# Where the long product of heads 0 and 1 stands in a visit's scores

## The chip, the cores and the metric

The kernel runs on one core of a Trainium2 chip. The metric is the time of one execution on the device in microseconds; lower is better. The engines are TensorE (PE in the profile, its weight loads PEld), VectorE (DVE), ScalarE (ACT), GpSimd (POOL) and SyncE (SP, which issues DMAs).

## The reference

```python
# x: (32, 256, 32, 32) float32, S = 1024 tokens, 8 heads of 32 channels
def reference(x, L0_conv_q_w, L0_conv_q_b, L0_conv_kv_w, L0_conv_kv_b):
    def _L0_conv_ref(x, q_w, q_b, kv_w, kv_b):
        ...
        q = jnp.einsum('oc,bcs->bos', q_w, xf) + q_b[None, :, None]
        kv = jnp.einsum('oc,bcs->bos', kv_w, xf) + kv_b[None, :, None]
        k, v = (kv[:, :EMBED_C], kv[:, EMBED_C:])
        ...
        mask = jnp.tril(jnp.ones((S, S), dtype=x.dtype), -int(MASK_CENTER))
        scores = jnp.einsum('bhqd,bhkd->bhqk', q, k) / jnp.sqrt(jnp.asarray(dk, x.dtype))
        scores = jnp.where(mask == 0, jnp.asarray(-10000.0, x.dtype), scores)
        attn = jax.nn.softmax(scores, axis=-1)
        attn = jnp.where(mask == 0, jnp.asarray(0.0, x.dtype), attn)
        out = jnp.einsum('bhqk,bhkd->bhqd', attn, v)
        ...
    # _gn: group norm over 32 groups of 8 channels
    x = x + _L0_conv_ref(_gn(x), L0_conv_q_w, L0_conv_q_b, L0_conv_kv_w, L0_conv_kv_b)
    return x
```

A group norm, three projections, strictly causal attention with 8 heads over 1024 tokens, and the residual, for 32 batch elements, all in float32.

## The kernel before

One element of the batch (called a batch below, b) has two groups g of four heads, and each group's attention is worked off in six visits i, so a batch has twelve visits, numbered v = 6g + i. A visit takes a part of the causal triangle: keys on the partitions, queries along the columns. `VISITS[i]` says which: one or two long products (rectangles, up to 512 queries wide) and, as a short one, either a pair of diagonal blocks (`pair`, in visits 0, 1, 3 and 4, which `PAIRS` lists) or one more rectangle of 256 queries (visits 2 and 5). Visits 0 and 5 have two long products, 384 and 128 wide; 1, 2, 3 and 4 have one, 512 wide. A pair consists of two products for each half of the keys, one 128 and one 64 wide.

The scores of one head have a contraction of only 32 channels, so `score` (L329, tile `sT`) uses a 32x64 part of the TensorE array: the rows of the array are the head's, and the two halves of a block's 128 keys go to different columns of it. Four heads and two halves are eight such parts. Each float32 matmul stands twice in the trace, as two passes. In all of the order's listings below, `x4` is two heads by two halves.

A visit has three PSUM tiles `sT`, numbered 0, 1 and 2 at the end of their names: 0 takes the long products of heads 0 and 1, 1 those of heads 2 and 3, and 2 the short products of all four, heads 2 and 3 in the same banks as heads 0 and 1. Two matmuls must not write one bank from different rows of the array at once, so the short products are made for heads 2 and 3 first, their last matmuls count up the semaphore `bank_free`, and TensorE waits for it ahead of the short products of heads 0 and 1.

The order is written out by hand (the pools and semaphores come from a tile framework, each engine's instructions stand as the code issues them): for each visit its scores, then parts of the projections (`pp`, `ppv`, L173), then the products with the values of the visit before (`acc`, L451). ScalarE takes the exponentials of the three `sT` tiles (L426, L426, L422) in the order 0, 1, 2; GpSimd masks the pairs; VectorE adds the exponentials up for the sums of the softmax.

In `scores` the list `begin` holds what is made of the long products of heads 0 and 1 before those of heads 2 and 3. `scores_of` calls its argument `between` between the first and the second product of a pair, and goes through the pair backwards (64 wide first) if told to by `order`. Before the change, `between` is used for heads 2 and 3 only where `begin` has more than one entry: in visit 0, whose two long products are two entries, and, in all batches but the last, in v = 3 and 4 (`SPLIT`), where `part_of` makes the one long product in two cuts of 128 and 384 queries. In the visits v = 1, 7, 9 and 10, and in 3 and 4 of the last batch, both products of the pair come first and then the long one.

Of the kernel before, what the change touches and what calls it, by code (L numbers as in the profile page):

```python
# [32 lines left out]
def tile_norm_attention_residual(  # L33
# [69 lines left out]
    def unshifted():  # L103
# [230 lines left out]
        def scores_of(b, g, bank_of, heads, entries, between=lambda: None, order=slice(None)):  # L334

            done = {}
            for _, _, halves in entries:
                for k, n in enumerate(list(range(max(map(len, halves))))[order]):
                    if k:
                        between()  # L340
                    for j in heads:
                        for c, ops in enumerate(halves):
                            if n < len(ops):
                                done.setdefault((j, c), []).append(score(b, g, bank_of(j), j, ops[n]))
            return done

        def part_of(b, g, bank, entry, of):

            at, _, halves = entry
            for j in (0, 1):  # L350
                for ((c, kb, first, _, cols),) in halves:
                    score(b, g, bank[:, j, :], j, (
                        c, kb, first + of.start, of.stop - of.start, slice(cols.start + of.start, cols.start + of.stop)
                    ))

        def mask(b, g, raw, j):


            hf, place = j // 2, (2 * j % 4) * P
            if ("e", b, g, "D", hf) not in live:  # L360
                live["e", b, g, "D", hf] = epool.tile(
                    [P, 4, HALF], F32, tag=("e0", "e")[hf], bufs=4, name=f"diagonal_{b}_{g}_{hf}"
                )
            square = live["e", b, g, "D", hf]
            for s in range(2):
                nc.gpsimd.affine_select(  # L366
                    out=square[:, :, place + s * P : place + (s + 1) * P],
                    in_=raw[:, :, (1 - s) * KEYS : (3 - s) * KEYS],
                    pattern=[[0, 4], [(1, -1)[s], P]], compare_op=ALU.is_gt, fill=0.0, base=0,
                    channel_multiplier=(-1, 1)[s],  # L370
                )
            if j == 0:
                nc.gpsimd.memset(square[0:1, :, 0:1], 1.0)

        def scores(b, v):


            g, i = divmod(v, len(VISITS))
            longs, shorts = VISITS[i]
            name = f"{b}_{g}_{i}"  # L380
            e = epool.tile([P, 4, HALF], F32, tag="e0" if i == TOTAL else "e", bufs=4, name=f"e_{name}")
            eh = epool.tile([P, 4, HALFBANK], F32, tag="eh", bufs=3, name=f"eh_{name}")
            pairs = [ps_s.tile([P, 2, HALF], F32, tag="sT", name=f"sT_{name}_{a}") for a in range(3)]
            short = pairs[2].rearrange("p bank (n q) -> p bank n q", n=2)
            short_of = lambda heads, *how: scores_of(
                b, g, lambda j: short[:, j % 2, j // 2, :], heads, shorts, *how
            )
            long_of = lambda heads, n: scores_of(b, g, lambda j: pairs[j // 2][:, j % 2, :], heads, longs[n : n + 1])
            rest = [lambda: long_of((2, 3), 1)] if len(longs) > 1 else []
            begin = [lambda n=n: long_of((0, 1), n) for n in range(len(longs) - 1, -1, -1)]  # L390
            if b < B - 1 and v in SPLIT:
                begin = [lambda n=n: part_of(b, g, pairs[0], longs[0], n) for n in (slice(0, P), slice(P, HALF))]
            if i in PAIRS and len(begin) > 1:
                first = short_of((2, 3), begin.pop(0), slice(None, None, -1))
            else:
                first = short_of((2, 3))
            for f in begin:
                f()
            long_of((2, 3), 0)

            ends = [made[-1] for made in first.values()]
            first = [ins for made in first.values() for ins in made]
            for ins in ends:
                ins.then_inc(bank_free, 1)
            for ins in first:
                tc.no_tile_sem_insts.add(ins.ins.name)
            live["free"] = live.get("free", 0) + len(ends)
            wait = nc.tensor.wait_ge(bank_free, live["free"])
            for ins in first:
                tc.declare_no_dep(wait.ins, ins.ins, reason="the semaphore orders them")  # L410
            made = short_of((0, 1), *rest if i in PAIRS else ())
            if i not in PAIRS:
                for f in rest:
                    f()
            for made in made.values():
                for lo in made:
                    for ins in first:
                        tc.declare_no_dep(lo.ins, ins.ins, reason="the semaphore orders them")
            wide, narrow = (max(at + width for at, width, _ in entries) for entries in (longs, shorts))
            for a in range(3):  # L420
                if a == 2:
                    exp = nc.scalar.activation(  # L422
                        eh.rearrange("p (n bank) q -> p bank n q", n=2)[:, :, :, :narrow], short[:, :, :, :narrow], AF.Exp
                    )
                else:
                    nc.scalar.activation(e[:, 2 * a : 2 * a + 2, :wide], pairs[a][:, :, :wide], AF.Exp)  # L426

            for ins in first:
                tc.add_to_no_dep_group(f"first_{name}", ins.ins)
                tc.add_to_no_dep_group("first", ins.ins)  # L430
            tc.declare_no_dep(exp.ins, group=f"first_{name}", reason="through the last two products")
            tc.declare_fence(exp.ins, group=f"first_{name}")
            live["e", b, g, "L", i], live["e", b, g, "H", i] = e, eh
            if i in PAIRS:
                mask(b, g, eh, PAIRS[i])
# [183 lines left out]
        ]  # L619
        N, TOTAL = NG * len(VISITS), 2  # L620
        PAIRS = {0: 0, 1: 1, 3: 3, 4: 2}
        SPLIT = 3, 4

        PRODUCTS = [
            (0, [
# [65 lines left out]
        with tc.manual_schedule(engines={ENG.PE, ENG.Activation, ENG.DVE, ENG.Pool, ENG.SP}):  # L691
# [47 lines left out]
            for b in range(B):  # L739
                first, last = b * N, b == B - 1  # L740
# [44 lines left out]
            for i in range(B * N + 1):  # L785
                if i < B * N:
                    scores(*divmod(i, N))
                for f in at.pop(i, ()):
                    f()
                b, v = divmod(i - 1, N)  # L790
                if i == B * N:

                    sums(3, SUMMED[v], False)
                if i:
                    for _ in range(EVEN.count((i - 1) % N) if i < B * N - N else 0):
                        nc.tensor.wait_ge(bank_free, live["free"])
                    values(b, v)
                    if b < B - 1 or v not in SUMMED or v == 1:
                        add_keys(b, v)
                if i in (B * N - 2, B * N - 1):  # L800

                    sums(3, SUMMED[v])
                for f in after.pop(i, ()):
                    f()
# [9 lines left out]
    def shifted():  # L814


        with ExitStack() as inner:
# [34 lines left out]
            with tc.For_i(0, B, 1) as b:  # L852
# [93 lines left out]
                )  # L946

    inside = unshifted()
    ALL = 3 * P * ROW
    held = nc.values_load(  # L950
# [29 lines left out]
```

## Time and profile before

| | us |
|---|---|
| median of 3 runs | 1791.41 (1791.25 to 1792.9) |
| the profiled execution, from its first instruction to its last | 1791.2 |
| TensorE busy in it | 1782.1 (99%) |
| VectorE busy | 1669.4 (93%) |
| ScalarE busy | 1441.4 (80%) |
| GpSimd busy | 897.9 (50%) |
| one batch in the middle (stretch 957.88 to 1012.86) | 54.98 |

The page gives no other time of the profiled execution than its span, which is 0.2 us below the median of the runs. Busy time of TensorE is the union of matmuls that overlap in the array, so 99% says that some matmul was always in flight, not that the array was full.

### The profile page before, as it was taken

Reading aid. Unit: us, or ns where it says so; the run is one execution under the profiler, and the core shown is the slowest. Engines: PE = TensorE matmul, PEld = TensorE weight load, DVE = VectorE, ACT = ScalarE, POOL = GpSimd, SP = SyncE. Lnnn points to the kernel's source line nnn. Section 1 sums busy time; section 2 is a strip of 40 time slices with the busy share of each in tenths; the row PEclk is TensorE's granted clock in tenths of the full one; section 3 lists DMA queues with packets and bytes.
Section 4 is the critical chain, followed back from the end, with each engine's and each line's share of the span. In section 5 each row is a group of like instructions: output and inputs, shape, how many; then the busy total and the mean of one; then the engine's idle time right before and its main releaser. Section 6 shows DMA issues by size and latency. Waiting matters only on the chain.

```text
span 1791.2 us, 81784 instructions
## 1 busy us (share of the span) xinstructions
PE 1782.1 (99%) x37036; PEld 936.1 (52%) x37036; DVE 1669.4 (93%) x1796; ACT 1441.4 (80%) x1928; POOL 897.9 (50%) x935
## 2 busy tenths in 40 slices
PE   9999999999999999999999999999999999999998
PEld 5555555555555555555555555555555555555554
DVE  4689999999999999999999999999999999999998
ACT  6888878888778788788887888877888878888785
POOL 2355554554555555545555555454455554554542
PEclk9999999999999999999999999999999999999999
DMA  2567766767677676676776676767766766777663
GB/s 72 105 117 142 137 133 135 148 138 147 128 142 138 137 141 138 132 144 142 142 138 134 137 142 138 150 129 140 139 145 131 141 136 135 149 138 141 133 109 98
DMA packets 92771, 240.21 MB, mean 134 GB/s; under 512 B 26272, under 2 KB 27792, under 8 KB 76544
## 3 DMA queue, kind: packets, MB, share of 16 engines
q0 software_dynamic: 17360, 100.58, 40.1%
q1 hardware_dynamic: 74912, 134.28, 25.9%
q8 instruction: 290, 4.75, 1.1%
q14 instruction: 65, 0.53, 0.1%
q10 hardware_dynamic: 144, 0.07, 0.0%
HBM read 69.90 MB, written 34.95 MB: 59 GB/s over the span
## 4 chain that ended last, share of the span: by engine, by line
PE 99%; DVE 0%; ACT 0%; issue 0%; POOL 0%; POOLq 0%
PE sT L329 31%; PE acc L451 28%; PE pp L173 27%; PE ppv L173 13%; PE pd L503 1%; PE busy L159 0%; PE wt L152 0%; ACT e L426 0%; DVE rb_last L576 0%; DVE rb_last L563 0%; DVE turned L560 0%; DVE acc L573 0%; DVE inv_last L562 0%; POOL ident masks.py:199 0%; PE pv L173 0%
## 5 line engine op out<-in xcount | busy, mean ns | idle before, releaser
L426 ACT ACTIVATE e<-sT 128x1024 f32<-128x1024 f32 x768 | 744.3, 1022 | 301.5 <-PE sT L329 298.8
L366 POOL TENSOR_SCALAR_AFFINE_SELECT diagonal<-eh 128x512 f32<-128x512 f32 x512 | 563.3, 1122 | 625.4 <-ACT eh L422 624.7
L469 DVE TENSOR_TENSOR e<-e,e 128x1024 f32<-128x1024 f32 x314 | 578.0, 1841 | 23.0 <-ACT v L293 3.5
L329 PE MATMUL sT<-q,k 32*64 32x64 f32 (+1 forms) x18928 | 577.9, 367 | 0.1
L329 PEld LDWEIGHTS sT<-q,k 32*64 32x64 f32 x18928 | 397.0, 131 | 203.8 <-PE sT L329 67.4
L173 PE MATMUL pp<-xn,wT 128*32 128x512 f32 x4096 | 492.3, 598 | 0.0
L451 PE MATMUL acc<-e,v 128*32 128x512 f32 (+3 forms) x4608 | 401.0, 450 | 0.0
L422 ACT ACTIVATE eh<-sT 128x768 f32<-128x768 f32 (+1 forms) x384 | 341.6, 890 | 0.0
L451 PEld LDWEIGHTS acc<-e,v 128*32 128x32 f32 x4608 | 149.2, 110 | 261.5 <-issue 239.0
L173 PE MATMUL ppv<-wT,xn 128*32 128x256 f32 x4096 | 247.5, 382 | 0.0
L469 DVE TENSOR_TENSOR diagonal<-diagonal,e 128x1536 f32<-128x1536 f32 x126 | 194.5, 1544 | 16.1 <-PE acc L451 6.5
L173 PEld LDWEIGHTS pp<-xn,wT 128*32 128x32 f32 x4096 | 107.0, 109 | 195.8 <-issue 163.7
L469 DVE TENSOR_TENSOR e<-e,eh 128x1024 f32<-128x1024 f32 x126 | 177.6, 1410 | 6.5
L451 PEld LDWEIGHTS acc<-diagonal,v 128*32 128x32 f32 x4096 | 120.9, 110 | 88.1 <-issue 68.2
L173 PEld LDWEIGHTS ppv<-wT,xn 128*32 128x32 f32 x4096 | 120.2, 109 | 80.0 <-issue 7.0
L469 DVE TENSOR_TENSOR e<-e,diagonal 128x2048 f32<-128x2048 f32 x63 | 144.0, 2285 | 18.9 <-POOL diagonal L366 18.7
L451 PE MATMUL acc<-diagonal,v 128*32 128x128 f32 x4096 | 158.9, 273 | 0.0
L205 POOL DMA_INDIRECT eight<-each,group_of x31 | 42.9, 1383 | 193.4 <-DMA each<-st 193.4
L262 ACT ACTIVATE xn<-x,shift,rstd 128x256 f32<-128x256 f32 x248 | 137.2, 614 | 0.8 <-POOL shift L247 0.8
L576 DVE SCALAR_TENSOR_TENSOR rb<-num,v_bias_col,x 128x256 f32<-128x256 f32 x248 | 121.5, 530 | 4.4
L482 POOL DMA_DIRECT2D e<-e x124 | 103.6, 835 | 42.6 <-issue 42.6
L482 POOL DMA_DIRECT2D diagonal<-diagonal x124 | 105.1, 847 | 0.7
(87 smaller groups left out, 1092.2 us busy)
## 6 DMA issues: line engine op xcount, KB each, us to landing
x<-in_x_dram SPq DMA_DIRECT2D x124, 256.0 KB, 3.8
diagonal<-diagonal POOLq DMA_DIRECT2D x62, 512.0 KB, 6.1
e<-e POOLq DMA_DIRECT2D x62, 512.0 KB, 5.7
rb<-inverses SPq DMA_DIRECT2D x124, 256.0 KB, 4.0
out_dram<-rb SPq DMA_DIRECT2D x124, 256.0 KB, 4.2
diagonal<-diagonal POOLq DMA_DIRECT2D x62, 256.0 KB, 4.6
folded<-diagonal SPq DMA_DIRECT2D x62, 256.0 KB, 5.1
e<-e POOLq DMA_DIRECT2D x62, 256.0 KB, 4.6
```

What stands on the lines that cost most here:

```text
L173: nc.tensor.matmul(out[part], lhsT=lhsT[:, part], rhs=rhs, start=start, stop=stop, skip_group_check=True)
L205: nc.gpsimd.indirect_dma_start(eight, None, live["each", b].rearrange("(m c) s -> m (c s)", c=CPG), bass.IndirectOffsetOnAxis(ap=group_of[ ...
L262: nc.scalar.activation(to, of, AF.Identity, bias=live["shift", b][:, g : g + 1], scale=rstd)
L329: return nc.tensor.matmul(bank[c : c + KEYS, cols], lhsT=live["k", b, g][rows, kb * P + c : kb * P + c + KEYS], rhs=live["q", b, g][rows, ...
L366: nc.gpsimd.affine_select(out=square[:, :, place + s * P : place + (s + 1) * P], in_=raw[:, :, (1 - s) * KEYS : (3 - s) * KEYS], pattern=[ ...
L422: exp = nc.scalar.activation(eh.rearrange("p (n bank) q -> p bank n q", n=2)[:, :, :, :narrow], short[:, :, :, :narrow], AF.Exp)
L426: nc.scalar.activation(e[:, 2 * a : 2 * a + 2, :wide], pairs[a][:, :, :wide], AF.Exp)
L451: nc.tensor.matmul(acc[HD * j : HD * (j + 1), of], lhsT=live["v", b][:, kb, h * HD : (h + 1) * HD], rhs=e[:, j, :], start=first, stop=last ...
L469: nc.vector.tensor_add(to, to, tile_of(b, g, at))
L482: nc.gpsimd.dma_start(out=total[:rows], in_=total[rows : 2 * rows], accum_op=ALU.add)
L503: nc.tensor.matmul(pd[HD * j : HD * (j + 1), of], lhsT=pick, rhs=e[:, j, :], start=start, stop=stop, skip_group_check=True,)
L576: nc.vector.scalar_tensor_tensor(blocks(rb, s), blocks(num, s, (start + s) % 2 == 1), v_bias_col[:, g : g + 1], blocks(xt[:, g, cols], s), ...
```

## The change

In every visit with one long product and a pair, the long product of heads 0 and 1 goes between the pair's two products for heads 2 and 3, in one piece of 512 queries. The pair is then gone through forwards, 128 wide first; with two long products (visit 0) backwards, as before. `SPLIT` becomes empty, so `part_of` isn't called.

```diff
             begin = [lambda n=n: long_of((0, 1), n) for n in range(len(longs) - 1, -1, -1)]
             if b < B - 1 and v in SPLIT:
                 begin = [lambda n=n: part_of(b, g, pairs[0], longs[0], n) for n in (slice(0, P), slice(P, HALF))]
-            if i in PAIRS and len(begin) > 1:
-                first = short_of((2, 3), begin.pop(0), slice(None, None, -1))
+            if i in PAIRS:
+                first = short_of((2, 3), begin.pop(0), slice(None, None, -1 if len(longs) > 1 else 1))
             else:
                 first = short_of((2, 3))
...
-        SPLIT = 3, 4
+        SPLIT = ()
```

On TensorE, visit 1 of a batch: names are tile, batch of the buffer, visit and tile number (the last number counts buffers); `sT_0_1_2` is tile 2, the short products. Before:

```order
L173 MATMUL pp_0_1_1_408<-xn_1_279,wT 32x512 x8
L329 MATMUL sT_0_1_2_422<-q_0_284,k_0_295 64x128 x4
L329 MATMUL sT_0_1_2_422<-q_0_284,k_0_295 64x64 x4
L329 MATMUL sT_0_1_0_420<-q_0_284,k_0_295 64x512 x4
L329 MATMUL sT_0_1_1_421<-q_0_284,k_0_295 64x512 x4
L329 MATMUL sT_0_1_2_422<-q_0_284,k_0_295 64x128 x4
L329 MATMUL sT_0_1_2_422<-q_0_284,k_0_295 64x64 x4
```

And after the change:

```order
L173 MATMUL pp_0_1_1_408<-xn_1_279,wT 32x512 x8
L329 MATMUL sT_0_1_2_422<-q_0_284,k_0_295 64x128 x4
L329 MATMUL sT_0_1_0_420<-q_0_284,k_0_295 64x512 x4
L329 MATMUL sT_0_1_2_422<-q_0_284,k_0_295 64x64 x4
L329 MATMUL sT_0_1_1_421<-q_0_284,k_0_295 64x512 x4
L329 MATMUL sT_0_1_2_422<-q_0_284,k_0_295 64x128 x4
L329 MATMUL sT_0_1_2_422<-q_0_284,k_0_295 64x64 x4
```

The long product of heads 0 and 1 (`sT_0_1_0`) has moved up past the 64-wide product of heads 2 and 3. On TensorE, visit 3, which was cut, before:

```order
L329 MATMUL sT_0_3_2_547<-q_0_284,k_0_295 64x64 x4
L329 MATMUL sT_0_3_0_545<-q_0_284,k_0_295 64x128 x4
L329 MATMUL sT_0_3_2_547<-q_0_284,k_0_295 64x128 x4
L329 MATMUL sT_0_3_0_545<-q_0_284,k_0_295 64x384 x4
L329 MATMUL sT_0_3_1_546<-q_0_284,k_0_295 64x512 x4
L329 MATMUL sT_0_3_2_547<-q_0_284,k_0_295 64x128 x4
L329 MATMUL sT_0_3_2_547<-q_0_284,k_0_295 64x64 x4
```

And after the change:

```order
L329 MATMUL sT_0_3_2_547<-q_0_284,k_0_295 64x128 x4
L329 MATMUL sT_0_3_0_545<-q_0_284,k_0_295 64x512 x4
L329 MATMUL sT_0_3_2_547<-q_0_284,k_0_295 64x64 x4
L329 MATMUL sT_0_3_1_546<-q_0_284,k_0_295 64x512 x4
L329 MATMUL sT_0_3_2_547<-q_0_284,k_0_295 64x128 x4
L329 MATMUL sT_0_3_2_547<-q_0_284,k_0_295 64x64 x4
```

The 128-wide and 384-wide cuts have become one product of 512, and the pair's order is turned round. Over the whole program TensorE has 62 rows fewer (3709 for 3771), one for each cut visit; the other engines have as many as before.

## The prediction

> **What bounds the kernel now.** I read the page first: the engines' totals and the chain of waits.
>
> ```profile
> span 1791.2 us, 81784 instructions
> PE 1782.1 (99%) x37036; PEld 936.1 (52%) x37036; DVE 1669.4 (93%) x1796; ACT 1441.4 (80%) x1928; POOL 897.9 (50%) x935
> PE 99%; DVE 0%; ACT 0%; issue 0%; POOL 0%; POOLq 0%
> L329 PE MATMUL sT<-q,k 32*64 32x64 f32 (+1 forms) x18928 | 577.9, 367 | 0.1
> ```
>
> The chain that ended last lies on TensorE for 99% of the span, and the score products (L329) were preceded by 0.1 us of idle time in all. So the kernel takes as long as TensorE's instruction stream takes, and the question is how closely the matmuls of one visit's scores can be packed. The second engine is VectorE. One batch in the undisturbed middle takes 54.98 us, of which VectorE is busy 52.70:
>
> ```profile
> 957.88:1012.86 54.98, 54.98 (x1156) 28.86 (x1152) 52.70 (x57) 44.94 (x61) 28.82 (x29) 1.00 0.71 139
> DVE mv L212 <- DMA eight<-each,group_of: 2.7, 1, 2.7
> ```
>
> (The first numbers are the stretch and its length, then the busy time of PE, PEld, DVE, ACT and POOL, and the granted clock, 1.00.) The second row, of the waits, is the one late transfer of this run; I come back to it as noise.
>
> Next the timeline of TensorE for four visits of batch 14, start and length of each merged group:
>
> ```profile
> 789.27 1.49 PE L329 MATMUL sT<-q,k 32*64 32x64 f32 x64
> 790.69 1.92 PE L173 MATMUL pp<-xn,wT 128*32 128x512 f32 x16
> 792.43 1.05 PE L451 MATMUL acc<-e,v 128*32 128x384 f32 x16
> 793.84 1.47 PE L329 MATMUL sT<-q,k 32*64 32x128 f32 x48
> 795.24 1.93 PE L173 MATMUL pp<-xn,wT 128*32 128x512 f32 x16
> 798.40 1.55 PE L329 MATMUL sT<-q,k 32*64 32x256 f32 x32
> 802.60 1.46 PE L329 MATMUL sT<-q,k 32*64 32x64 f32 x56
> 803.99 0.64 PE L173 MATMUL ppv<-wT,xn 128*32 128x256 f32 x8
> ```
>
> The scores groups are visit 0 (789.27, two long products), visit 1 (793.84, plain order), visit 2 (798.40, no diagonal pair) and visit 3 (802.60, cut in two). After each the next product starts about 0.07 us before the scores' last matmul ends: 789.27+1.49 against 790.69, 793.84+1.47 against 795.24, 802.60+1.46 against 803.99. So what a visit's scores cost is the length from the first score matmul's start to the last one's end, and a nanosecond off that length is a nanosecond off the span. Ten nanoseconds of resolution are too few here, so I summed that length over 60 visits of one kind in batches 1 to 30, one stretch around each visit; first row and sum of each answer (visits 1 and 10; 3 and 4; 2 and 8; 0 and 6):
>
> ```profile
> 78.02:79.74 1.72, 1.47 (x48) 1.00 0.00 0
> sum 103.39, PE 88.42; mean PE 1.47
> ```
>
> ```profile
> 86.77:88.48 1.71, 1.46 (x56) 1.00 1.00 216
> sum 102.44, PE 87.43; mean PE 1.46
> ```
>
> ```profile
> 82.57:84.37 1.80, 1.55 (x32) 1.00 0.04 9
> sum 107.75, PE 92.74; mean PE 1.55
> ```
>
> ```profile
> sum 104.35, PE 89.37; mean PE 1.49
> ```
>
> Divided by 60: a plain visit 1473.7 ns, a cut one 1457.2, visit 2 1545.7, visit 0 1489.5.
>
> **The change part by part.** I call the parts of a visit with a pair and one long product S128 and S64 (the wide and the narrow first products of heads 2 and 3), L01 and L23 (the long products), and T (the diagonal products of heads 0 and 1). Plain visits run S128, S64, L01, L23, T; the cut ones S64, L01's first 128 columns, S128, L01's other 384, L23, T. The change makes both S128, L01, S64, L23, T. There are 6 such visits in each of 32 batches: 62 cut ones (visits 3 and 4 of all but the last batch) and 192-62 = 130 plain ones.
>
> Where does a plain visit lose time? I cut the first 80 ns of visits 1, 2 and 3 into three slices and counted the score matmuls that run in each (number after x):
>
> ```profile
> 793.84:793.87 0.02, 0.02 (x4) 1.00 0.05 0
> 793.87:793.89 0.02, 0.02 (x4) 1.00 0.48 102
> 793.90:793.92 0.02, 0.02 (x8) 1.00 0.06 0
> 798.40:798.42 0.02, 0.02 (x4) 1.00 0.00 0
> 798.43:798.45 0.02, 0.02 (x8) 1.00 0.00 0
> 802.60:802.62 0.02, 0.02 (x4) 1.00 0.00 0
> 802.63:802.65 0.02, 0.02 (x8) 1.00 0.00 0
> ```
>
> Four matmuls (two heads, two halves of the keys) go out per slice of about 27 ns. In visits 2 and 3, where the long product of heads 0 and 1 stands second, its matmuls run in the second slice; in the plain visit, where it stands third, S64's place goes by with nothing started and L01 appears in the third. Which matmuls those are, the shapes running 0.10 to 0.15 us into visit 1 tell:
>
> ```profile
> L329 PE MATMUL sT<-q,k 32*64 32x512 f32 x4 | 0.7, 638 | 0.0
> L329 PE MATMUL sT<-q,k 32*64 32x128 f32 x4 | 0.3, 318 | 0.0
> ```
>
> S128 and L01 run side by side, on different rows of the array; no 64-wide matmul runs yet, S64 waits for its rows behind S128. So L01 loses one slot of issue to a product that could not start then. L01 and T share rows, and their chain ends a plain visit: of the two rows below (shapes still running 1.43 to 1.46 us into visit 1) the score matmuls are 64 wide, T's last, and L23 is over. In the cut visit, 1.453 to 1.457 us in, a single 512-wide matmul of L23 is what still runs:
>
> ```profile
> L173 PE MATMUL pp<-xn,wT 128*32 128x512 f32 x4 | 0.6, 617 | 0.0
> L329 PE MATMUL sT<-q,k 32*64 32x64 f32 x4 | 0.2, 217 | 0.0
> ```
>
> ```profile
> L329 PE MATMUL sT<-q,k 32*64 32x512 f32 x1 | 0.6, 587 | 0.0
> L173 PE MATMUL ppv<-wT,xn 128*32 128x256 f32 x4 | 0.4, 403 | 0.0
> ```
>
> - Moving L01 ahead of S64. L01 starts one slot, 27 ns, earlier, and T follows L01 on its rows, so a plain visit should go from 1473.7 to about 1447 ns. S64's rows are taken by S128 until long after its new slot, so it starts when it did, and L23 behind it too: L23 was over before 1.43 us and leaves about 17 ns to 1447 at worst.
> - Bounds of that gain. Below: if L23's end is stretched as in the cut visits, the visit ends at 1457.2, a gain of 16.5. Above: visit 2 has the new shape (long product second) with 64 columns more on each row. Four rounds of 512 columns take 792.43-790.69 = 1.74 us, 0.85 ns a column; two passes of 64 columns are 109 ns, and 1545.7-109 = 1437, a gain of 37. But T is in two pieces where visit 2 has one, two more starts of matmuls a row, so I take 27, the slice, which is nearest to the thing itself.
> - Uncutting L01 in 62 visits. One matmul of 512 replaces 128 and 384; these visits become the same as the others, 1447 instead of 1457.2, a gain of 10. The cut visits start L01 in the second slot already, so no 27 here; what they can gain is L23's end, which is late in them for a reason that these rows don't tell. Between 0 (it stays late) and 20 (1457.2-1437).
> - The semaphore. T must wait until S64 and S128 are done (same banks). In visit 1 the next weights after L23's load about 0.75 us in, and T's matmuls start at 0.96 (below: from 0.56 to 0.72 us after the start no weights are loaded, then four, and the T matmuls come after 0.96):
>
> ```profile
> 794.40:794.56 0.16, 0.16 (x13) 0.00 (x0) 0.00 (x0) 1.00 0.09 13
> 794.59:794.80 0.21, 0.21 (x12) 0.12 (x4) 0.00 (x0) 1.00 0.07 10
> 794.80:794.83 0.03, 0.03 (x16) 0.02 (x4) 0.00 (x0) 1.00 0.00 0
> ```
>
>   With T 27 ns earlier this wait still ends some 0.15 us ahead of need. If S64 slipped by more than that, T would be late.
> - The wait of L01 for its bank now stands ahead of S64, on the exponentials of the visit before. Behind it queue S64 and L23. Visit 2 has the same wait in the same place and starts in its second slice, so it costs nothing.
> - No instruction of ACT, VectorE, GpSimd or SyncE moves against its neighbours, and no DMA. ACT gets L01 some 27 ns sooner; VectorE has 2.3 us of idle time a batch, and the batch becomes 0.13 us shorter. The cover is kept.
>
> Sum: 130 x 27 = 3.5 us, 62 x 10 = 0.6 us, 4.1 us together, from 1791.2 to 1787.1 in the span. The median of the runs, 1791.41, is 0.2 above the span; 1787.2 is the forecast for it. All bounds low: 130 x 16.5 = 2.1, 1789.3. All high: 130 x 37 + 62 x 20 = 6.0, 1785.4.
>
> A rule speaks against this. The Trainium skill (TensorE: Matmul & The Clock Gate, Step-by-step: what each phase is for) says that weight loads are pulled ahead but the matmuls themselves stay in program order; by it S64 could not start before L01's passes had been issued, and the sum would be a loss of some 36 us (the second rival works the same delay out from rows). The rows above differ: in visit 1 L01 runs while S64, which stands before it, has not begun.
>
> **The rivals.**
>
> 1. *L23's end decides.* The new order gives every visit the end of a cut one, 1457.2: 1789.3, no measurable change (0.2%, 3.6 us, is about what a measurement of this kernel can tell). For it: the cut visits have L01 second and end on L23. Against: visit 1's L23 ended early. 10%.
> 2. *Program order across rows, slower.* S64 is held behind L01's second pass. L01 has 512 columns a pass, 0.435 us, so S64 would start at about 0.51 us instead of 0.27 (two passes of S128 at 109 ns and the first start's 0.05). L23 follows 0.24 later, of which about 0.05 is slack: +0.19 us on each of 192 visits, 36 us, 1828. It turns slower once S64 slips by more than the 17 to 50 ns of slack. Against: the shapes at 0.10 us. 4%.
> 3. *The interleaving disturbs itself, as in visit 0.* That visit has as many columns and an interleaved order, and takes 1489.5: 130 x 16 + 62 x 32 = 4.1 us more, 1795.5. It has two more pieces, though, and its long products are cut. 4%.
> 4. *The slot is not the cause*, and all become like plain visits: cut ones lose 16.5 x 62 = 1.0, 1792.4. For it: L01's later start could be its wait for a bank; against: visit 2 has the wait and no delay. 9%.
>
> **How the numbers follow.** My forecast has 73%. Around it lies noise of about 1 us: the three runs spread over 1.65 us, and the late transfer of 2.7 us above can come once more or not at all. The range 1785.2 to 1789.6 holds the forecast, its bounds and rival 1, 83% less the noise, about 8 in 10. Faster by over 0.2% means below 1787.83, only 0.6 above the forecast: 0.8 of 73% and a few of rival 1's make 0.60; slower, rivals 2 and 3, 0.08; the same 0.32.
>
> **What would show it.** In the profile after: four matmuls in the first slice and eight in the second in every such visit; a length of 1447 ns for visits 1, 3, 4, 7, 9 and 10 alike; no form of 384 columns left in visits 3 and 4; T's 64-wide matmuls the last to end. A length near 1457 with L23 last says rival 1; 64-wide matmuls that start after 0.5 us say rival 2; L01 in the third slice says rival 4. I would be wrong altogether if VectorE or ACT turned up in the chain of waits.

## The result, and the profile after

The changed kernel takes 1882.1 us (median of 4 runs, 1879.5 to 1884.79) for 1791.33 before: 1.0506 times as long, 95% interval 1.0491 to 1.0521. I had forecast 1787.2 and a range up to 1789.6. The page of its profiled execution, and the waits of TensorE's weight loads before (first row) and after (second):

```profile
span 1880.9 us, 80792 instructions
PE 1869.3 (99%) x36540; PEld 915.9 (49%) x36540; DVE 1655.0 (88%) x1796; ACT 1461.7 (78%) x1928; POOL 848.3 (45%) x935
PE 99%; DVE 0%; DMA 0%; issue 0%; ACT 0%; SPq 0%
```

```profile
PEld sT L329 <- PE sT L329: 67.4, 381, 0.2
```

```profile
PEld sT L329 <- PE sT L329: 192.5, 384, 0.8
```

TensorE still carries the chain, and still counts as busy 99% of it. The row that grew by far the most is that of the weight loads of the scores that wait for other score matmuls: 381 waits of at most 0.2 us became 384 of up to 0.8. The timeline of visits 1 and 2 of batch 14, the slices of visit 1 as in the prediction, and the shapes that run 0.27 to 0.29 us into it:

```profile
831.49 1.93 PE L329 MATMUL sT<-q,k 32*64 32x128 f32 x48
833.35 1.92 PE L173 MATMUL pp<-xn,wT 128*32 128x512 f32 x16
...
836.50 1.54 PE L329 MATMUL sT<-q,k 32*64 32x256 f32 x32
```

```profile
831.49:831.51 0.02, 0.02 (x4) 1.00 0.00 0
831.52:831.54 0.02, 0.02 (x8) 1.00 0.00 0
831.54:831.56 0.02, 0.02 (x8) 1.00 0.00 0
```

```profile
L329 PE MATMUL sT<-q,k 32*64 32x512 f32 x4 | 0.7, 638 | 0.0
L329 PE MATMUL sT<-q,k 32*64 32x128 f32 x8 | 0.4, 293 | 0.0
L329 PE MATMUL sT<-q,k 32*64 32x64 f32 x4 | 0.2, 214 | 0.0
```

Everything that I expected of the start of a visit is there: L01 runs in the second slice, and S64's four matmuls start 0.27 us in, beside it. Then follows a stretch in which no weights of the scores are loaded. The columns below are the stretch, its length, and the busy time and number of score matmuls, weight loads and ACT instructions:

```profile
832.05:832.21 0.16, 0.16 (x13) 0.00 (x0) 0.00 (x0) 1.00 0.00 0
832.21:832.85 0.64, 0.64 (x12) 0.00 (x0) 0.18 (x1) 1.00 0.00 0
832.85:832.89 0.04, 0.04 (x8) 0.03 (x4) 0.04 (x1) 1.00 0.00 0
```

T's weights are loaded 1.37 us after the visit's start, not 0.73 to 0.75. Visit 2, 1.54 us, is as before. Summed over the same 60 visits as in the prediction (1 and 10, then 3 and 4):

```profile
sum 131.00, PE 116.02; mean PE 1.93
```

```profile
sum 131.00, PE 116.03; mean PE 1.93
```

That is 1933.7 ns a visit: 460 more than a plain one had, 476.6 more than a cut one. 130 x 0.460 + 62 x 0.4766 = 89.3 us; the spans differ by 1880.9-1791.2 = 89.7. So the longer visits are the whole of the change, to within 0.4 us.

### The profile page after: what moved, and what is told of

Same layout as the page of the kernel before. It is cut to its first block, busy times and chain, and to the rows that moved or that the text cites. A ratio compares the mean times of both kernels' runs of the same rounds, so it can differ in the third digit from the quotient of the medians.

```text
span 1880.9 us, 80792 instructions
## 1 busy us (share of the span) xinstructions
PE 1869.3 (99%) x36540; PEld 915.9 (49%) x36540; DVE 1655.0 (88%) x1796; ACT 1461.7 (78%) x1928; POOL 848.3 (45%) x935
## 4 chain that ended last, share of the span: by engine, by line
PE 99%; DVE 0%; DMA 0%; issue 0%; ACT 0%; SPq 0%
PE sT L329 34%; PE acc L451 26%; PE pp L173 25%; PE ppv L173 13%; PE pd L503 1%; DMA x<-in_x_dram 0%; PE wt L152 0%; ACT e L426 0%; DVE st L189 0%; DVE rb_last L576 0%; DVE rb_last L563 0%; PE busy L159 0%; SPq L111 0%; DVE turned L560 0%; DVE acc L573 0%
## 5 line engine op out<-in xcount | busy, mean ns | idle before, releaser
L366 POOL TENSOR_SCALAR_AFFINE_SELECT diagonal<-eh 128x512 f32<-128x512 f32 x512 | 509.4, 1015 | 759.1 <-ACT eh L422 754.2
L329 PE MATMUL sT<-q,k 32*64 32x128 f32 (+2 forms) x18432 | 665.9, 374 | 1.2 <-issue 0.9
L469 DVE TENSOR_TENSOR e<-e,e 128x1024 f32<-128x1024 f32 x314 | 560.7, 1786 | 27.0 <-PE acc L451 7.7
L329 PEld LDWEIGHTS sT<-q,k 32*64 32x64 f32 x18432 | 376.9, 131 | 314.1 <-PE sT L329 192.5
L469 DVE TENSOR_TENSOR diagonal<-diagonal,e 128x1536 f32<-128x1536 f32 x126 | 188.1, 1493 | 16.1 <-PE acc L451 6.3
L469 DVE TENSOR_TENSOR e<-e 128x512 f32<-128x512 f32 x64 | 57.9, 904 | 109.6 <-ACT q L276 108.4
L576 DVE SCALAR_TENSOR_TENSOR rb<-num,v_bias_col,x 128x256 f32<-128x256 f32 x248 | 127.4, 554 | 4.4
```

Source lines behind the costliest of these rows:

```text
L329: return nc.tensor.matmul(bank[c : c + KEYS, cols], lhsT=live["k", b, g][rows, kb * P + c : kb * P + c + KEYS], rhs=live["q", b, g][rows, ...
L366: nc.gpsimd.affine_select(out=square[:, :, place + s * P : place + (s + 1) * P], in_=raw[:, :, (1 - s) * KEYS : (3 - s) * KEYS], pattern=[ ...
L469: nc.vector.tensor_add(to, to, tile_of(b, g, at))
L576: nc.vector.scalar_tensor_tensor(blocks(rb, s), blocks(num, s, (start + s) % 2 == 1), v_bias_col[:, g : g + 1], blocks(xt[:, g, cols], s), ...
```

## The experiments

The semaphore events in the trace tell the rest. In visit 1 of batch 14 the four counts (increments) of `bank_free` come 0.555, 0.597, 0.640 and 0.682 us after the visit's start before the change, and 1.201, 1.244, 1.286 and 1.329 after it, 42 to 43 ns apart in both. The signal that L01 is complete, on which ACT's first exponential waits, comes at 1.184 before, behind the counts, and at 1.159 after, 42 ns ahead of the first of them. L23's signal comes at 1.466 and 1.467, so the counts don't wait for that one. From this came the **theory**: S64 is done as early as before, but completions are signalled in program order, so S64's counts now stand behind L01's completion. The **rival**: running L01 beside the pair, or a whole L01 as such, holds up the results or T itself.

**The cut taken away alone** (before, with `SPLIT = ()`).

> Before, with only the cutting of visits 3 and 4 taken away: S128, S64, L01 whole, L23, T everywhere. Theory (the semaphore's counts for S64 are given out in program order, behind L01's completion): nothing stands between S64 and its counts, so T starts 0.96 us into the visit and these 62 visits become plain ones, 1474 ns for 1457: +1.0 us, 1792.4. Rival (a whole L01 of 512 columns beside the pair is what is slow): 62 visits take 0.46 us more, +28 us, 1820.

Measured: 1798.08 us, 1.0035 times before (1.0024 to 1.0046). The visits 3 and 4:

```profile
sum 103.40, PE 88.42; mean PE 1.47
```

1473.7 ns, the plain visits' value to the nanosecond: a whole L01 beside the pair doesn't hold up T, and the rival's 28 us are out. The expected 1.0 us is there; the other 5 or so aren't in the lengths of ordinary visits and are taken up further down.

**One first product, ahead of L01.**

```diff
-                first = short_of((2, 3), begin.pop(0), slice(None, None, -1 if len(longs) > 1 else 1))
+                if len(longs) > 1:
+                    first = short_of((2, 3), begin.pop(0), slice(None, None, -1))
+                else:
+                    first = scores_of(
+                        b, g, lambda j: short[:, j % 2, j // 2, :], (2, 3),
+                        [(at, width, [
+                            [(c, kb, shorts[0][2][0][0][2], 3 * KEYS, slice(at, at + 3 * KEYS))] for (c, kb, *_), _ in halves
+                        ]) for at, width, halves in shorts],
+                    )
```

> The changed kernel, but S128 and S64 of heads 2 and 3 are one product of 192 columns that stands ahead of L01 (other queries, so that these two heads' diagonal blocks aren't the reference's; the same number of columns is streamed). Theory: the counts stand ahead of L01 in program order, come some 0.57 us into the visit, T starts at about 0.94 us, and a visit takes the 1447 ns that was predicted: 1787.2, 94 us below the changed kernel. Rival (L01 running beside the pair holds up the pair's results or T): nothing is gained, about 1881.

Measured: 1788.15 us, 0.9979 times before (0.9970 to 0.9988), span 1786.8. The visits 1 and 10, and T's weights in visit 1 (none from 0.56 to 0.715 us, four from 0.716 to 0.750):

```profile
sum 101.80, PE 86.82; mean PE 1.45
```

```profile
791.42:791.58 0.15, 0.15 (x12) 0.00 (x0) 0.00 (x0) 1.00 0.00 0
791.58:791.62 0.03, 0.03 (x8) 0.03 (x4) 0.00 (x0) 1.00 0.00 0
```

86.82/60 is 1447.0 ns, what the prediction had worked out, with L01 in the second slot and the same columns to stream (heads 2 and 3 have one matmul fewer for each half of the keys, since the two products are one). With the counts ahead of L01 in program order, the last comes at 0.676 us. The gain that the prediction spoke of exists; it was the place of the counts that turned it over.

**How much of L01 stands ahead of the counts.** In three kernels L01 is cut again, the first piece standing between S128 and S64:

```diff
-            if b < B - 1 and v in SPLIT:
-                begin = [lambda n=n: part_of(b, g, pairs[0], longs[0], n) for n in (slice(0, P), slice(P, HALF))]
+            if i in SPLIT:
+                begin = [lambda n=n: part_of(b, g, pairs[0], longs[0], n) for n in (slice(0, P), slice(P, HALF))]
...
-        SPLIT = ()
+        SPLIT = 1, 3, 4
```

(and with `2 * P` or `3 * P` for `P`).

> The changed kernel with L01 cut into 128 and 384: S128, 128 columns of L01, S64, 384 columns of L01, L23, T. Theory: the counts wait only for the first 128 columns of L01, which are done before S64 is; T starts at about 0.94 us, and L23's end is not stretched, since its weights no longer load together with those of L01's second cut: about 1452 ns a visit, 130 x 22 + 62 x 5 ns = 3.2 us less than before, 1788.1. Rival (S64 standing behind a piece of L01 makes the counts late): between before and the changed kernel, over 1792.

> As cut_between, but L01 is cut into 256 and 256, so that S64's counts stand behind 256 columns of L01. Theory (counts in program order, behind the completion of that piece, 42 ns apart): the piece's second pass streams until about 0.53 us, its completion comes some 0.17 us later, the four counts at 0.74 to 0.87, T's weights load at about 0.91, T begins some 25 ns late, and a visit takes about 1474 ns: 1792.4, as good as before. Rival (counts wait for all of L01): about 1881.

> As cut_between, but with L01 cut into 384 and 128. Theory: the piece of 384 streams until about 0.74 us, the last count comes at about 1.08, T's weights load at 1.13, and a visit takes about 1690 ns: 130 x 0.216 + 62 x 0.233 = 42 us more than before, 1834. Rival (counts wait for all of L01): about 1881. Rival (the length of the piece does not matter): as cut_between.

Measured: 1819.03, 1819.15 and 1841.47 us, 1.0148, 1.0145 and 1.0273 times before. The stretch in which T's weights are first loaded in visit 1, for 256 and for 384 columns (the stretch ahead of it has none):

```profile
803.96:804.19 0.23, 0.23 (x13) 0.00 (x0) 0.00 (x0) 1.00 0.00 0
804.19:804.22 0.03, 0.03 (x12) 0.03 (x4) 0.00 (x0) 1.00 0.00 0
```

```profile
812.22:812.46 0.25, 0.25 (x20) 0.00 (x0) 0.00 (x0) 1.00 0.26 66
812.47:812.50 0.03, 0.03 (x9) 0.03 (x4) 0.00 (x0) 1.00 0.00 0
```

Together, in us from the start of visit 1 of batch 14, from semaphore events and the starts of loads and matmuls:

| columns of L01 ahead of S64 | last count | T's weights | T's first matmul |
|---|---|---|---|
| 0 (before, plain) | 0.682 | 0.726 | 0.962 |
| 0 (one product) | 0.676 | 0.718 | 0.937 |
| 128 | 0.702 | 0.744 | 0.941 |
| 256 | 0.877 | 0.919 | 0.942 |
| 384 | 1.089 | 1.131 | 1.133 |
| 512 (the change) | 1.329 | 1.370 | 1.372 |

From 256 columns on, each 128 more put off the counts by 0.21 to 0.24 us, two passes of 128 columns at 109 ns each; T's weights follow the last count by 41 to 44 ns in every row; T itself is late only once that moment passes the end of L01. The cut of 384 gave T at 1.133 where 1.13 was expected, and a visit of 1694.5 ns (101.67/60, visits 3 and 4) where 1690 was; the whole time lies 7 us above the expected 1834.

The times of the first two kernels were missed, though, by 31 and 27 us. The visits 3 and 4 of `cut_between`, and the shapes of its visit 1 that still run at 1.50 us and that run at 0.41 to 0.455:

```profile
sum 108.66, PE 93.63; mean PE 1.56
```

```profile
L173 PE MATMUL pp<-xn,wT 128*32 128x512 f32 x4 | 0.6, 617 | 0.0
L329 PE MATMUL sT<-q,k 32*64 32x512 f32 x3 | 0.6, 588 | 0.0
```

```profile
L329 PE MATMUL sT<-q,k 32*64 32x512 f32 x1 | 0.6, 590 | 0.0
L329 PE MATMUL sT<-q,k 32*64 32x384 f32 x4 | 0.5, 481 | 0.0
L329 PE MATMUL sT<-q,k 32*64 32x128 f32 x8 | 0.3, 268 | 0.0
L329 PE MATMUL sT<-q,k 32*64 32x64 f32 x8 | 0.3, 216 | 0.0
```

T is on time there, but three of L23's four matmuls start at 0.46 to 0.50 us instead of 0.39 to 0.40, and end the visit at 1560.5 ns: their weights are loaded only from 0.458 us on, 131 ns after those of the first. That isn't all of the miss: from the lengths of ordinary visits `cut_between` would be 130 x 86.8 + 62 x 103.3 ns = 17.7 us above before, and its span is 29.5 above. The other 12 us, like 9 in `cut_half` and 5 in `cut_wide`, aren't in ordinary visits; all three have stops of TensorE, of which more below.

**L23 ahead of the second cut.** `long_of((2, 3), 0)` is issued before the cut of 384.

> cut_between with the second cut of L01 issued after L23: S128, 128 columns of L01, S64, L23, 384 columns of L01, T. In cut_between three of L23's four weight loads came 0.13 us late, with the second cut of L01 between S64 and L23. Theory A (that order makes them late): here L23 starts at 0.38 us as in the plain order and is over before 1.43 us; L01's second cut starts late instead, at about 0.41 to 0.46, T at about 1.05 to 1.1, a visit takes 1560 to 1610 ns. Theory B (any cut of L01 makes L23 late): L23 starts at 0.46 again and ends the visit at 1560 or later. Both lie above before; about 1810 to 1830.

Measured: 1839.48 us, 1.0262 times before. At 0.41 to 0.455 us now all four of L23 run, and one of the cut's:

```profile
L329 PE MATMUL sT<-q,k 32*64 32x512 f32 x4 | 0.6, 590 | 0.0
L329 PE MATMUL sT<-q,k 32*64 32x384 f32 x1 | 0.5, 481 | 0.0
```

So theory A has the right product late: whichever long product is issued second after the pair gets three of its four weights late, here the cut (0.293 us for the first, 0.459 on for the others), and with it most of T, whose first matmul starts at 0.990 and the others from 1.100 on. Its size was missed: a visit takes 1681 ns, 71 above the expected range, and the whole time lies some 10 us above. Why they load late isn't shown by any run.

**One count instead of four.** `ends` keeps its last entry alone, and `with_scores` waits for one count a visit.

> The changed kernel with one count of the semaphore instead of four in every visit: only the last matmul of S64 (in visits 0, 2 and 5 of the last short product of heads 2 and 3) counts. Theory: the four counts come 42 ns after one another behind L01's completion, so T's weights load 3 x 42 = 126 ns earlier, 192 x 0.126 = 24 us less than the changed kernel: 1857. Rival (the late moment is set by L01's or L23's end alone, not by the counts themselves): no difference, 1881.

Measured: 1869.16 us, 1.0434 times before; 12.9 us less than the changed kernel. T's weights in visit 1 (none from 0.56 to 1.29 us, four from 1.291 to 1.320):

```profile
827.44:828.17 0.73, 0.73 (x17) 0.00 (x0) 0.11 (x1) 1.00 0.00 0
828.17:828.20 0.03, 0.03 (x8) 0.03 (x4) 0.03 (x1) 1.00 0.00 0
```

The count comes at 1.251 and the weights at 1.293, 77 ns earlier, 192 x 0.077 = 15 us. That the counts are in the path is so shown; that leaving out three of them saves 3 x 42 ns isn't: L01's completion comes at 1.159 as in the changed kernel, so 92 ns remain between it and the single count.

**The cut order in every visit**, and **visit 0 in the new form**.

> Before, with its cut order (S64, 128 columns of L01, S128, 384 columns of L01, L23, T) in all six visits with a pair and one long product, of all batches. Theory: the first cut has completed long before S128, so the counts aren't late, and 130 plain visits become cut ones: 130 x 16.5 ns = 2.1 us less, 1789.2. Rival (interleaving costs by itself): slower than 1791.3.

> cut_between, and visits 0 and 6 put into the same form: pair forwards, the 128-wide long product of heads 0 and 1 between, then all of the long products, then T uninterrupted (before: pair backwards, and the 128-wide long product of heads 2 and 3 between T's two). Theory: a visit 0 goes from 1490 ns to the 1452 of cut_between: 64 x 37 ns = 2.4 us less than cut_between, 1785.7. Rival (visit 0 is long for the number of its pieces, not for their order): as cut_between, within 0.3 us.

Measured: 1796.85 us (1.0027, 1.0016 to 1.0037) and 1822.22 us (1.0167). `cut_all`'s visits have the expected 1457 ns (87.41/60 for visits 3 and 4), yet the kernel is 5 us slower: the rival's time came, but not by longer visits. Its trace has four idle stretches of TensorE in its scores for which the profile names nothing that it waited for, 2.0 us in all, and seven waits of VectorE for the norm's gathered sums, 13.4 us, where before had none of the first and one of the second. In `both_kinds` visits 0 and 6 went from 1489.5 to 1567 ns, by L23's late weights, as in `cut_between`.

**Stops outside the visits' own length.** `uncut_only`, too, shows idle time of TensorE that before had none of (waits of TensorE; four times, 0.9 us at most):

```profile
PE sT L329 <- issue: 2.6, 4, 0.9
```

One of them, in batch 22, on the timeline, and the DMA queues of that core in the 7.6 us that end 0.42 us before the visit, and in the 1.4 us after them:

```profile
1235.55 1.42 PE L329 MATMUL sT<-q,k 32*64 32x128 f32 x40
1237.74 0.34 PE L329 MATMUL sT<-q,k 32*64 32x64 f32 x8 [0.76 <-issue]
```

```profile
q0 software_dynamic: 111, 0.65, 58.8%
q1 hardware_dynamic: 104, 0.38, 19.2%
```

```profile
q1 hardware_dynamic: 80, 0.13, 32.8%
q8 instruction: 1, 0.02, 5.5%
```

TensorE waits for nothing that the profile shows, and a transfer of the instruction queue, of which there was none in the stretch ahead, starts 2.6 us before it goes on.

> uncut_only with 128 waits on TensorE that are already fulfilled, put in once near the start, so that every later instruction lies 128 places further in the program. uncut_only was 5 us slower than its visits explain; its trace has stops of TensorE of up to 1.1 us, each about 2.4 us after a 16 KB transfer of the instruction queue that came 8 to 11 us after the one before. Theory (where the program's pieces for loading instructions begin decides where TensorE runs dry): the stops move, and the time changes by more than 1 us, to between 1792 and 1796. Rival (the stops come from the order of the products): the same visits stop, 1798 plus some 2 us for the waits.

> Before with the same 128 fulfilled waits on TensorE near the start. Theory (place in the program decides): before has hardly a stop of that kind, and moved by 128 places it gets some: 1794 to 1800. Rival (the order decides, and before's has none): 1791.4 plus at most 2 us for the waits themselves, and no stops in the trace.

Measured: 1808.45 us (1.0087) and 1805.7 us (1.0086). Both are spoilt for their times: the 128 waits cost a stop of 6.7 us at the start (`wt`, L152), and the first scores begin some 8 to 9 us later. What can be read is the place of the stops. `uncut_only` has idle stretches of this kind in batches 5, 10, 14, 22 and 31, `uncut_shift` in 7, 12, 13, 16 and 24: they moved, as expected. `before_shift` got none, though the theory said that it would; it got 14 waits of VectorE for the norm's gathered sums where before had one, and three more scores lengthened by 0.4 to 0.7 us (visit 11 of batches 5, 12 and 18):

```profile
DVE mv L212 <- DMA eight<-each,group_of: 23.1, 14, 3.7
```

The traces of the other runs add something. `cut_between` and `cut_half` have these waits of TensorE:

```profile
PE sT L329 <- issue: 4.8, 8, 1.0
```

```profile
PE sT L329 <- issue: 2.5, 5, 0.9
```

Four of the five of `cut_half`, and both of `cut_wide`, of `long_last` and of `both_kinds`, lie in visits in which `cut_between` has one (visit 1 of batches 9, 17, 21 and 29, visit 7 of 26 and 30). All of these kernels have equally many matmuls in their traces, 38076. So a change of the program need not move the stops. But `cut_all` has as many matmuls, too, and its four lie in other visits, so the place in the program doesn't settle it alone. The stops of `uncut_only`, `uncut_shift` and `cut_between` all end 2.2 to 2.9 us after an instruction transfer of 16 KB that came 8.0 to 10.6 us after the one before it; yet in the trace before, between 60 and 1720 us, 28 such transfers come over 8 us after the one before, and TensorE stops at none of them. That the stops are late loads of instructions is what the queue suggests, and isn't shown.

## Why the prediction was wrong

- *What bounds the kernel*: right. A nanosecond of a visit's scores was a nanosecond of the span, up and down: 89.3 us by visits for 89.7 of span in the changed kernel, and 4.1 for 4.4 in `one_first`.
- *L01 ahead of S64*: right to the nanosecond. L01 started a slot earlier, S64 when it did, and where T wasn't held up a visit took 1447.0 ns (`one_first`, with S128 and S64 made as one product; the changed kernel without its wait was not run).
- *Uncutting L01*: right under its condition. By itself it costs 16.5 ns a visit (`uncut_only`, 1473.7); with L01 second and T on time it gives the 10 that were forecast (`one_first`, 1447.0 in visits 3 and 4 too). The reason for which L23 ends late in the cut visits, which the prediction left open, can be followed one step in the trace before: in visit 3 of batch 14 three of L23's four weight loads come 77 ns after the first (0.278 and 0.355 us) and 16 ns apart, its second passes start 16 to 22 ns apart instead of 6 to 7, and the last ends at 1.457.
- *The semaphore*: this is the step that failed. It took the time at which S64 ends for the time at which its counts come, found 0.15 us in hand (the weights that it read as loading at 0.75 us start at 0.726, which makes it 0.21), and asked only whether S64 itself could slip. S64 didn't; its counts came 0.65 us later, because L01, which now stands ahead of it, completes at 1.16 us, and T was 0.41 us later than before. The other 0.05 us of the 0.46 lie in T's own start: its weights had been loaded well ahead of its matmuls, at 0.73 for 0.96, and now its first matmuls go out with them, and its second matmuls follow 160 ns after the first instead of 109.
- *The rule set aside.* The Trainium skill (TensorE: Matmul & The Clock Gate, Step-by-step: what each phase is for) keeps matmuls in program order. Of starts that is not what the traces show, before or after: L01 runs ahead of S64 in the one (0.053 against 0.269 us), S64 and L23 ahead of L01's second pass in the other (0.269 and 0.384 against 0.507). Of the signals of completion it is: the last count comes at 0.676 to 1.329 us by how much of L01 stands ahead. I weighed the rule against starts and dropped it whole.
- *The rivals*: rival 2 had program order as the cause, but in the wrong place (it holds S64's start there), and 36 us for it; the others didn't come about. In the kernel before no count stood behind a long product: in the cut visits only 128 columns of L01 stand ahead of the product that counts. So the trace before could not show what the counts do behind 512 columns, and that wait should have been bounded from both sides instead of being taken from S64's end.

## What to carry to other kernels

In these runs a matmul that overtook another in the array did not signal ahead of it, which put T's wait off by 0.65 us. Before moving a long instruction past a short one whose semaphore somebody waits for, price the wait as if the short one ended after the long one. Put the products that others wait for ahead of the long ones in program order, or let only a piece stand ahead that is over sooner. And when a change of 0.1% is looked for, compare the visits' own lengths as well as the whole time: the kernels here differ by up to 12 us that isn't in ordinary visits, and single stops of up to 1 us are part of it.

## What the runs showed of the hardware

- On different rows of the array, matmuls start out of program order (before, L01 at 0.053 us, beside S128, while S64, issued ahead of it, starts at 0.269). Semaphore updates come in program order (after, L01's at 1.159, S64's at 1.201 to 1.329), those of consecutive matmuls 42 to 43 ns apart, and a weight load that waited for the last of them starts 41 to 44 ns after it.
- With two long products issued behind a pair, three of the four weight loads of the later one come late, whichever product that is: 131 ns after the first where it is L23 (0.327 and 0.458 us in `cut_between`), 166 ns where it is the cut (0.293 and 0.459 in `long_last`), 77 ns in the cut visits before. It isn't settled why.
- TensorE stood idle for 0.2 to 1.0 us at a time for no reason that the waits show. 128 waits put in near the start moved these stops (`uncut_only`, `uncut_shift`); some changes of the order left them in the same visits (`cut_between`, `cut_half`, `cut_wide`). It isn't settled what decides.
